# Gram-Schmidt rounds in the first half of each feed-forward pass, additions row by row, and a later turn in the last pass

## The chip, the cores and the metric

The kernel runs on one core of one Trainium2 chip. The metric is the device time of one execution in microseconds. The core has five engines with a queue of instructions each: TensorE (PE in the profile, with its weight loads as PEld), VectorE (DVE), ScalarE (ACT), GpSimd (POOL) and SyncE (SP). An engine takes its instructions in order; one that waits on a semaphore holds all behind it. DMAs are issued from a queue too, here nearly all from SP, a few from POOL. All arithmetic is in float32.

## The reference, cut to what matters

Eight sequences of 512 tokens with 512 features go through four layers:

```python
x = L0(x, ...)   # finite differences on a 512x512 grid, relu
x = L1(x, ...)   # attention with bias, then a feed-forward of 2048:
    h = _ln(x) * g2 + beta2
    ff = _gelu2(h @ W1 + b1) @ W2 + b2;      return x + ff
x = L2(x, ...)   # a feed-forward with weights of one expert per sequence:
    h = gelu(x @ Wi_b + bi_b);  r = h @ Wo_b + bo_b + x;  y = layernorm(r) * g_b + be_b
x = L3(x, ...)   # a low-rank edit:
    U_o = gram_schmidt(U);  V_o = gram_schmidt(V)      # U, V: 512 x 32
    basis = U_o @ V_o.T
    ...                                                # gate from the mean over tokens
    feats = (x @ basis) @ basis.T[:, :32]
    return x + strength * (feats @ resp_w.T + resp_b + safety_bias)
```

`gram_schmidt` is sequential over its 32 columns: column i is normalized, then its projection is taken from all later columns.

## The kernel before, in words

**Stages.** The grid of layer 0 takes the first 150 us or so, the attention of layer 1 runs to 1075 us, and then come sixteen feed-forward passes (`NQ = 2 * NB`): pass q = 0 to 7 is layer 1's feed-forward for sequence q, pass q = 8 to 15 is layer 2's expert feed-forward for sequence q - 8, followed by layer norm and layer 3 (the "tail"), most of which is done inside the next pass. The change is all in the feed-forward stage, `mlp_stage` (L1198).

**One pass.** A 128-partition tile `x` of 4 rows (R = 4) by 512 holds a sequence. Both matrix products of a pass are done with a seven-product scheme in place of eight block products, so that sums and differences of weight blocks (`w_quads`, `t13`, `t2s2`, `t4s4`, `r_sum`, on POOL by way of `gadd`) and of activation blocks (`b_staged`, `s13`, `l_sum`, on DVE by way of `add`, one operand staged into PSUM by ACT) have to be ready before the products that use them. `run(q, hooks)` (L1594) writes the pass:

- slots 0 to 27: four groups g of seven products u (slot 7g + m). Each is 8 matmuls of 128x256 into one of six PSUM buffers of tag `u`. The first product of a group is copied out by ACT, the others are added by DVE; then ACT applies the GELU, `gelu(1)` after product 5 and `gelu(0)` after product 6.
- slots 28 to 35 and 40 to 43: `second`, products y over all four groups. The first of them (y_28) reads, for group g, the first half of that group's activations, which `gelu(0)` writes; so its last 8 matmuls read what `gelu(0)` of the last group wrote.
- slots 36 to 39 and 44 to 55: `third`, four products split once more (named p2, p7, p3, p4, their tiles y_36, y_44, y_48, y_52). y_52a needs the DVE sums of p4, made at slots 47 to 49. In the last pass the fourth is replaced by two plain products, 52 and 54, each followed by `last_row`.

**The order is written by hand.** `hooks` maps a slot to a list of functions; `at(hooks, s, f, ...)` (L2139) appends one, and `go(s)` runs the list when the loop comes to that slot, before its matmuls. Every instruction is pinned to program order, so slot and place in the list set where it stands in each engine's queue. Hooks registered first stand first: at slots 7 and 14, `w_quads` is registered ahead of whatever Gram-Schmidt hook has the same slot.

**Gram-Schmidt.** The rows 0 to 31 of a 64x512 tile `qm` hold U transposed, rows 32 to 63 V transposed. Thirty-two rounds, four in each of passes 0 to 7, work on both at once:

- `gs_a(i)` (L1255): two DMAs on POOL's queue spread row i of either half over 32 partitions, into a tile `qb` (two buffers). 64 KB each.
- `gs_norm(i)` (L1265): on DVE two products with sums, of qb with itself (`junk_gn`) and of qm with qb (`junk_gd`), L1236; on POOL a square root as a power (L1243).
- `gs_b(i)` (L1270): on DVE the reciprocal (L1250, L1252), the coefficients `al` (L1275, L1276), the update of `qm` (L1277); and then it calls `gs_a(i + 1)`.

So round i + 1 can't begin before the DMAs of row i + 1 have landed, and these wait for the update of round i. After pass 7, `low_rank` (pass 8, slots 5 to 20) makes the low-rank weights of layer 3 out of `qm`.

**The rest that the change touches.** `add_row` (L1408) adds a bias row to all four rows of x on POOL. `add_beta` (L2023) adds layer 3's bias times the gate to a finished sequence in the tail, on POOL, and `tail_add` adds the response after it. `tail_turn` (L1969) turns 128 columns of the last pass's first two rows with two PE transposes and copies them out with ACT (L1983); the rows were scaled by DVE (L1934) at slot 50.

Of the kernel before, what the change touches and what calls it, by code (L numbers as in the profile page):

```python
# [22 lines left out]
D = 512  # L23
P = 128
R = 4
# [14 lines left out]
def fused_kernel(ctx: ExitStack, tc: tile.TileContext, a: dict):  # L40
# [172 lines left out]
    def load_late():  # L213
# [7 lines left out]
        g2, mhalf, load_w, load_late,  # L221
    )
    mlp_stage(tc, a, small, xp, io, wo8, x1d, ident, eidx, sigs, layernorm, rstd_of, phalf, wl3, g2, b1, first)


# [972 lines left out]
def mlp_stage(tc, a, small, xp, io, wo8, x1d, ident, eidx, sigs, layernorm, rstd_of, phalf, wl3, g2, b1, first):  # L1198
# [4 lines left out]
    with ExitStack() as ctx:  # L1203
# [15 lines left out]
        def gadd(out, x, y, op=ALU.add):  # L1219
            pin(nc.gpsimd.tensor_tensor(out, x, y, op))  # L1220
# [128 lines left out]
        wis, wos, xs, bts, tbs, wss, extra = {}, {}, {}, {}, {}, {}, {}  # L1349
# [57 lines left out]

        def add_row(q):  # L1408
            row = b2 if q < NB else extra[q][1][0]
            gadd(xs[q], xs[q], row[:, None, :].to_broadcast([P, R, D]))  # L1410

        hs, norms = {}, {}

# [26 lines left out]
        def rows32(q, r, src):  # L1440

            if r == 0:
                blks[q] = w8(wo8, f"tt_{q}").rearrange("p k d -> p (k d)").rearrange(
                    "p (n c r j) -> p c n r j", c=2, r=R, j=RK
                )
            pin(
                nc.vector.transpose(
                    blks[q][:, :, :, r, :], src.rearrange("p (c n j) -> p c n j", c=2, j=RK)
                )
            )  # L1450
# [572 lines left out]
        def add_beta(q):  # L2023
            x, st, beta = xs[q], outs[q]["st"], extra[q][1][2]
            pin(nc.vector.scalar_tensor_tensor(beta, rb, st, beta, ALU.mult, ALU.add))
            gadd(x, x, beta[:, None, :].to_broadcast([P, R, D]))

        def tail_sum(q, r):
            ft, m = outs[q]["ft"], slice(r * RK, (r + 1) * RK)
# [109 lines left out]
        def at(hooks, s, f, *args):  # L2139
            hooks.setdefault(s, []).append(lambda: f(*args))  # L2140
# [8 lines left out]
        for q in range(NQ):  # L2149
            hooks = {}  # L2150
            nx = q + 1 if q + 1 < NQ else None

            if q:
                at(hooks, 0, load_wi, q, 2)
                at(hooks, 0, load_wi, q, 3)
                at(hooks, 1, w_quads, q, 1, gadd)
            at(hooks, 0, load_wo, q)
            if nx:
                if nx >= NB:
                    at(hooks, 45, load_extra, nx)  # L2160
                at(hooks, 2, load_x, nx)
                at(hooks, 48, load_wi, nx, 0)
                at(hooks, 52, load_wi, nx, 1)
            if 1 <= q <= NB:
                at(hooks, 4, lambda q=q: nc.sync.dma_start(x2d[q - 1], xs[q - 1]))

            at(hooks, 2 if q else 26, add_row, q)
            at(hooks, 7, w_quads, q, 2, gadd)
            at(hooks, 14, w_quads, q, 3, gadd)
            for g in range(NG):  # L2170
                at(hooks, 18 + 2 * g, t13, q, g)
            if nx:
                if nx < NB:
                    at(hooks, 29, norm, nx)
                    at(hooks, 31, normed, nx)
                for r in range(R):
                    at(hooks, 34 + r, lambda r=r, n=nx: rows32(
                        n, r, hs[n][r] if n < NB else xs[n][:, r, :]
                    ))
                at(hooks, 38 if q <= NB else 40, turn, nx)  # L2180
                if nx < NB:
                    for c in range(KC):
                        at(hooks, 46 + c, scale, nx, c)
                at(hooks, 51, b_staged, nx)
                at(hooks, 51, w_quads, nx, 0, gadd)
            if q < NB:
                for i, s in enumerate((11 if q else 18, 25, 46, 51)):
                    at(hooks, s, gs_norm, 4 * q + i)
                    at(hooks, s + 2, gs_b, 4 * q + i)
            if q == 0:  # L2190
                at(hooks, 8, gs_a, 0)
                at(hooks, 10, load_constants)
                at(hooks, 38, constants)
            if q == NB:
                for i, s in enumerate((5, 11, 14, 16, 20)):
                    at(hooks, s, low_rank, i)
            elif q > NB:
                every = range(R)
                o = q - 1
                at(hooks, 5, tail_norm, o, every)  # L2200
                at(hooks, 9, tail_normed, o)
                for r in range(R):
                    at(hooks, 14 + 2 * r, lambda r=r, o=o: rows32(o, r, xs[o][:, r, :]))
                at(hooks, 28, tail_spread, o)
                for c in range(KC):
                    at(hooks, 34 + c, tail_scale, o, c)
                at(hooks, 37, tail_gamma, o, every)
                at(hooks, 38, tail_feats, o, every)
                at(hooks, 39, gate, o)
                at(hooks, 41, strength, o)  # L2210
                at(hooks, 42, add_beta, o)
                for r in range(R):
                    at(hooks, 46, tail_sum, o, r)
                    at(hooks, (47, 48, 49, 51)[r], tail_add, o, r)
            if q == NQ - 1:
                half = range(0, 2)
                at(hooks, 49, tail_norm, q, half)
                at(hooks, 50, tail_normed, q)
                for c in range(KC):
                    at(hooks, (51, 52, 53, 53)[c], tail_turn, q, half, [c])  # L2220
            run(q, hooks)


# [86 lines left out]
```

## Time and profile before

| | us |
|---|---|
| three runs | 2647.16, 2648.96, 2650.07 (median 2648.96) |
| the profiled execution | 2648.46 |
| its span, first to last instruction | 2646.5 |
| feed-forward stage | 1075 to the end |
| a pass with Gram-Schmidt (second and third) | 94.97 |
| the first pass | 102.4 (1074.94 to 1177.38) |
| pass 8 | 98.8 (1842.14 to 1940.95) |
| passes 9 to 14 | 97.67 each |
| in the third pass, busy: PE / DVE / ACT / POOL | 94.32 / 71.22 / 36.31 / 73.43 |

How to read it: "busy" is the time in which an engine worked; in the timelines an entry gives start, length, engine, line, operation, tiles written <- read, and in brackets how long the engine was idle just before and what ended that. In the waits "A x <- B y: total, times, longest" says that engine A waited before writing x for what B wrote in y. The page's slices show PE at nine tenths or more from the second slice on and a granted clock of nine tenths or more in all but the last; the mean granted clock is 0.994.

### The profile page before, as it was taken

The page shows a single profiled execution, that of the slowest core. Times are in us where ns is not written, and L with a number is a line of the kernel's source. Part 1 is how long each engine was busy: PE and PEld are TensorE (multiplying, and loading weights), DVE is VectorE, ACT ScalarE, POOL GpSimd, SP SyncE. Part 2 cuts the span into 40 slices and gives each one's busy share as a digit, 9 for nine tenths or more (in the row PEclk, how much of TensorE's full clock was granted, in tenths as well). Part 3 has the DMA queues.
Part 4 walks back from the last instruction along what each step waited for, and adds up shares of the span by engine and source line. Part 5 has one row for each costly group of instructions (what it writes and reads, how often), then busy time and mean ns, then how long its engine had stood idle before and what let it go on. Part 6 is the DMA issues. An engine that isn't in the chain of part 4 may idle for free.

```text
span 2646.5 us, 44047 instructions
## 1 busy us (share of the span) xinstructions
PE 2593.9 (98%) x15664; PEld 1968.5 (74%) x15664; DVE 1993.3 (75%) x3919; ACT 1311.1 (50%) x2748; POOL 1733.2 (65%) x1351
## 2 busy tenths in 40 slices
PE   6999999999999999999999999999999999999998
PEld 3455555555555555789899899898899899899897
DVE  7978898888888656587777777777667667667666
ACT  2676767777677766233334334333334434434433
POOL 4555565656555655478777777877776776776773
PEclk9999999999999999999999999999999999999998
DMA  9765766676666554543553563464245356256240
GB/s 327 255 228 184 263 199 232 216 242 220 238 222 227 174 188 166 142 137 96 166 180 68 152 197 74 128 189 138 108 161 179 108 184 199 89 187 214 74 174 34
DMA packets 241839, 460.59 MB, mean 174 GB/s; under 512 B 33904, under 2 KB 77496, under 8 KB 232534
## 3 DMA queue, kind: packets, MB, share of 16 engines
q1 hardware_dynamic: 237754, 447.04, 49.6%
q0 software_dynamic: 3552, 10.72, 3.8%
q8 instruction: 125, 2.05, 0.3%
q14 instruction: 92, 0.75, 0.1%
q10 hardware_dynamic: 316, 0.03, 0.0%
HBM read 398.43 MB, written 55.09 MB: 171 GB/s over the span
## 4 chain that ended last, share of the span: by engine, by line
PE 88%; DVE 7%; DMA 3%; issue 1%; ACT 1%; SPq 0%; POOL 0%; DVEq 0%; POOLq 0%; ACTq 0%
PE u L1211 28%; PE y L1211 12%; PE tr L564 8%; PE s L561 5%; PE ctx L561 4%; PE pv L561 4%; PE o L561 4%; PE pk L561 4%; PE pq L561 4%; PE y_36a L1211 2%; PE y_52a L1211 2%; PE y_36b L1211 2%; PE y_52b L1211 1%; PE y_44a L1211 1%; PE y_48a L1211 1%
## 5 line engine op out<-in xcount | busy, mean ns | idle before, releaser
L998 POOL TENSOR_TENSOR bt<-bt,mk 128x1024 f32<-128x1024 f32 x256 | 541.7, 2140 | 58.9 <-DMA bt<-in_bias 38.8
L1026 ACT ACTIVATE bt<-bt,mn 128x512 f32<-128x512 f32 x512 | 365.7, 718 | 80.1 <-DVE mn L1021 79.9
L564 PEld LDWEIGHTS tr<-ident,bt 128*128 128x128 f32 x2048 | 229.8, 141 | 149.4 <-issue 101.3
L1217 DVE TENSOR_TENSOR act<-u,u 128x512 f32<-128x512 f32 x256 | 175.4, 688 | 216.5 <-PE u L1211 186.0
L1021 DVE CUSTOM_DVE_ANT_0 bt<-s,bt 128x512 f32<-128x512 f32 x512 | 329.9, 684 | 4.7 <-PE s L561 4.1
L1211 PE MATMUL u<-bt,wi 128*128 128x256 f32 x1440 | 330.6, 379 | 0.0
L1052 ACT COPY pt<-tr 128x512 f32<-128x512 f32 x376 | 207.6, 584 | 204.9 <-PE tr L564 197.2
L1211 PEld LDWEIGHTS u<-bt,wi 128*128 128x128 f32 x1440 | 272.9, 190 | 35.9
L564 PE MATMUL tr<-ident,bt 128*128 128x128 f32 x2048 | 276.9, 278 | 7.6 <-ACT pt L1052 3.1
L1211 PE MATMUL u<-tb,ws 128*128 128x256 f32 x1024 | 242.3, 380 | 1.8 <-DVE yw L1217 1.8
L1211 PE MATMUL y<-t,s 128*128 128x256 f32 x1024 | 227.9, 380 | 0.0
L1211 PEld LDWEIGHTS u<-tb,ws 128*128 128x128 f32 x1024 | 194.6, 190 | 28.4 <-issue 2.1
L1211 PEld LDWEIGHTS y<-t,s 128*128 128x128 f32 x1024 | 193.2, 191 | 25.0
L1740 ACT ACTIVATE act<-act,b 128x512 f32<-128x512 f32 x128 | 85.3, 714 | 248.3 <-DVE act L1217 191.8
L1740 ACT ACTIVATE act<-act,bi 128x512 f32<-128x512 f32 x128 | 84.5, 713 | 239.0 <-DVE act L1217 239.0
L1050 DVE COPY pt<-tr 128x512 f32<-128x512 f32 x136 | 93.7, 689 | 134.8 <-PE tr L564 134.2
L1217 DVE TENSOR_TENSOR u<-u,u 128x512 f32<-128x512 f32 x192 | 131.3, 684 | 49.2 <-PE u L1211 48.2
L561 PE MATMUL s<-kt,qt 32*128 32x512 f32 x1024 | 165.7, 643 | 1.2 <-ACT kt L651 0.8
L1220 POOL TENSOR_TENSOR q<-wo,q 128x512 f32<-128x512 f32 x126 | 160.6, 1274 | 4.4
L1220 POOL TENSOR_TENSOR t<-wo,t 128x512 f32<-128x512 f32 x64 | 80.9, 1279 | 100.9 <-PE y L1211 100.9
L1502 ACT COPY st_s<-act 128x512 f32<-128x512 f32 x192 | 112.0, 589 | 70.4 <-DVE s L1217 32.2
L1220 POOL TENSOR_TENSOR wo<-wo 128x512 f32<-128x512 f32 x111 | 141.1, 1271 | 8.7
(440 smaller groups left out, 5575.5 us busy)
## 6 DMA issues: line engine op xcount, KB each, us to landing
bt<-in_bias SPq DMA_DIRECT2D x256, 512.0 KB
wo<-in_W SPq DMA_DIRECT2D x32, 1024.0 KB
wi<-in_Wi SPq DMA_DIRECT2D x32, 1024.0 KB
wo<-in_Wo_e SPq DMA_DIRECT2D x32, 1024.0 KB
wi<-in_W SPq DMA_DIRECT2D x28, 1024.0 KB
td<-tt SPq DMA_DIRECT2D x22, 1024.0 KB
bt<-td SPq DMA_DIRECT2D x176, 128.0 KB
gq<-coef_q SPq DMA_DIRECT2D x21, 512.0 KB
```

The lines of the kernel that those rows point to most:

```text
L561: pin(nc.tensor.matmul(out, lhsT=lhsT, rhs=rhs, start=start, stop=stop))
L564: pin(nc.tensor.transpose(out, src, ident))
L998: nc.gpsimd.tensor_tensor(bt, bt, mask[b, r][:, None, :].to_broadcast([P, 2, S]), ALU.add)
L1021: nc.vector.tensor_tensor_reduce(bt[:, i, :], ss[h], bt[:, i, :], -1.0, 3.0e38, ALU.add, ALU.min, mn)
L1026: nc.scalar.activation(bt[:, i, :], bt[:, i, :], AF.Exp, bias=mn, scale=-1.0, accum_out=sums[b, c][:, h, r : r + 1],)
L1050: pin(nc.vector.tensor_copy(pt[:, :, r % 2, :], tr))
L1052: pin(nc.scalar.copy(pt[:, :, r % 2, :], tr))
L1211: pin(nc.tensor.matmul(out, lhsT=lhsT, rhs=rhs, start=start, stop=stop))
L1217: pin(nc.vector.tensor_tensor(out, x, y, op))
L1220: pin(nc.gpsimd.tensor_tensor(out, x, y, op))
L1502: pin(nc.scalar.copy(t, parts[0]))
L1740: nc.scalar.activation(acts[:, g, k, :], acts[:, g, k, :], func, bias=bi[:, j : j + 1])
```

## The change

Three things are changed, and no arithmetic. (1) The four Gram-Schmidt rounds of a pass, which began at slots 11 (18 in pass 0), 25, 46 and 51 with `gs_b` two slots later, begin at 4 (6 in pass 0), 12, 17 and 23 with `gs_b` at 7 (9), 14, 19 and 25. In pass 0 the first `gs_a` goes from slot 8 to 1. (2) `add_row` and `add_beta` add four rows of 128x512 in place of one 128x2048, and `add_row` of pass 0 goes from slot 26 to 3. (3) In the last pass the four `tail_turn`s go from slots 51, 52, 53, 53 to 52, 53, 54, 55.

```diff
         def add_row(q):
             row = b2 if q < NB else extra[q][1][0]
-            gadd(xs[q], xs[q], row[:, None, :].to_broadcast([P, R, D]))
+            for r in range(R):
+                gadd(xs[q][:, r, :], xs[q][:, r, :], row)
...
         def add_beta(q):
             x, st, beta = xs[q], outs[q]["st"], extra[q][1][2]
             pin(nc.vector.scalar_tensor_tensor(beta, rb, st, beta, ALU.mult, ALU.add))
-            gadd(x, x, beta[:, None, :].to_broadcast([P, R, D]))
+            for r in range(R):
+                gadd(x[:, r, :], x[:, r, :], beta)
...
-            at(hooks, 2 if q else 26, add_row, q)
+            at(hooks, 2 if q else 3, add_row, q)
             at(hooks, 7, w_quads, q, 2, gadd)
             at(hooks, 14, w_quads, q, 3, gadd)
...
             if q < NB:
-                for i, s in enumerate((11 if q else 18, 25, 46, 51)):
+                for i, (s, e) in enumerate(((4, 7) if q else (6, 9), (12, 14), (17, 19), (23, 25))):
                     at(hooks, s, gs_norm, 4 * q + i)
-                    at(hooks, s + 2, gs_b, 4 * q + i)
+                    at(hooks, e, gs_b, 4 * q + i)
             if q == 0:
-                at(hooks, 8, gs_a, 0)
+                at(hooks, 1, gs_a, 0)
...
             if q == NQ - 1:
                 half = range(0, 2)
                 at(hooks, 49, tail_norm, q, half)
                 at(hooks, 50, tail_normed, q)
                 for c in range(KC):
-                    at(hooks, (51, 52, 53, 53)[c], tail_turn, q, half, [c])
+                    at(hooks, 52 + c, tail_turn, q, half, [c])
```

On the engines' queues the instructions of PE, ACT and DVE are the same in number; POOL has four additions for one in 23 places. On POOL's queue a pass from 1 to 7 now reads: w_quads 1, four row additions, power of round 0, w_quads 2, two DMAs, power of round 1, w_quads 3, two DMAs, power of round 2, t13 of group 0, two DMAs, t13 of groups 1 and 2, power of round 3, t13 of group 3, two DMAs.

## The prediction

> **What bounds the kernel now.** I read the page first, then the waits by engine, then the timelines of one ordinary pass (the third, 1272.35 to 1367.32), of the first pass, and of the last 50 us.
>
> ```profile
> PE 2593.9 (98%) x15664; PEld 1968.5 (74%) x15664; DVE 1993.3 (75%) x3919; ACT 1311.1 (50%) x2748; POOL 1733.2 (65%) x1351
> ```
>
> PE is the bound: 52.6 us of idle in the whole span, so a gain can only come out of the few PE waits, while a new PE wait is paid in full. The waits of PE in the feed-forward stage are these:
>
> ```profile
> PE y_52a L1211 <- DVE q L1217: 6.2, 8, 1.6
> ...
> PE y L1211 <- ACT act L1740: 2.6, 1, 2.6
> ...
> PE u L1211 <- DVE yw L1217: 1.8, 1, 1.8
> ...
> PE ytr L1214 <- DVE x L1934: 1.5, 1, 1.5
> PE y_44a L1211 <- DVE q L1217: 1.2, 1, 1.2
> ```
>
> The first is 1.63 in pass 0 and 0.65 in each of passes 1 to 7, the passes with Gram-Schmidt rounds; passes 8 to 15 don't have it. The second is in pass 0, the third at the start of pass 8, the fourth in the last pass.
>
> How a round is chained shows on POOL and DVE in the third pass (start, length, engine):
>
> ```profile
> 1316.99 0.95 POOL L1243 TENSOR_TENSOR gs_d<-gn_s,phalf 64x1 f32<-64x1 f32 x1 [3.02 <-DVE gn_s L1236]
> ...
> 1321.50 1.04 POOL L1259 DMA_DIRECT2D qb<-qm  x2 [1.08 <-DVE qm L1277]
> ...
> 1360.08 1.06 POOL L1259 DMA_DIRECT2D qb<-qm  x2 [5.59 <-DVE qm L1277]
> ```
> ```profile
> 1320.46 0.74 DVE L1277 SCALAR_TENSOR_TENSOR qm<-qb,al,qm 64x512 f32<-64x512 f32 x1
> ...
> 1367.73 0.68 DVE L1236 CUSTOM_DVE_ANT_0 junk_gn<-qb 64x512 f32<-64x512 f32 x1 [1.48 <-DMA qb<-qm]
> ```
>
> Issued at 1360.08, the row broadcast was usable at 1367.73: 7.65 us, with DVE standing still before it. For the broadcast issued at 1297.49 the tile view of qb gives
>
> ```profile
> DMA to landing us min/median/max: 4.6/5.2/5.7
> ```
>
> where 5.7 belongs to the second DMA, issued 0.54 later: 6.25 us from first issue to usable. Over all rounds it is 6.25 to 8.7 (1834.90 to 1843.61), the longer ones while weights are loading.
>
> **The deadline.** The last 8 matmuls of y_28 need the GELU of the last group's first half. Here it runs at 1321.84 and PE comes to them at 1320.70 + 5.18 = 1325.88. I count from a pass's first matmul (T = 1272.35): PE needs them at T+53.5. After the last round's gs_norm starts, the order on DVE is: gs_norm 1.22, u2 0.6, two s13 sums 1.2, u3 0.6, gs_b 1.51, two adds 1.2, one add 0.6; then on ACT two GELUs 1.33 and one 0.67, with 0.1 of handing over twice: 9.1. So **the fourth round's row must be there by T+44.4**, or PE waits.
>
> **Part 1, the rounds.** Removed: two rounds (2 x (1.22 + 1.51) on DVE) from slots 46 to 53 and the stand for the row at 51. Then the p4 sums end near T+87.2 (1362.3 less 2.7), before y_52a asks at T+88.6. All y_52a waits go: -6.2, of which 0.65 per pass 1 to 7. The start of pass 8 is no longer behind a late DVE: -1.8 (its 1.76 idle).
>
> Added: four rounds chained in slots 4 to 25. On POOL's queue each round is pow, then whatever stands before the two DMAs; at slots 7 and 14 w_quads is listed ahead of gs_b, so four gadds (4 x 1.235 = 4.94) come between pow and the DMAs; at slot 19 it is one t13 (2.5). Also, ops of DVE with two SBUF inputs were held while POOL worked: L1276 took 5.01 and 1.24 beside 0.15, L1277 1.72 beside 0.74, each until a POOL instruction ended. So:
> - Round 0: POOL has w_quads 1 from about T-1 (pass 9's row, 1939.91) and the four row adds until T+8.9; gs_norm at 7.6, held to about 8.85; pow until 10.6; w_quads 2 until 15.5. gs_b can start after the add of u_0_6, T+12.75; al held to 14.3, qm to 15.5, done 16.2. DMA 16.3, weight loads still running (here 0.69 to 1.05 busy until T+30): row there at 22.0 to 23.9, take 22.6. DVE comes to gs_norm at 21.95: almost no wait.
> - Round 1: pow ends at +1.7 (24.3), w_quads 3 then delays the DMAs to 29.3 without holds, 30.0 with them; row at 30.0 + 6.25 = 36.2. DVE stands for it from 31.2: 5 us, which the six u buffers cover (u_2_3 is read at 38.05, its buffer is wanted at slot 23, T+39.7; slack 1.7).
> - Round 2: 1.22, u3 0.6, two adds 1.2, gs_b 1.51 plus a hold to t13's end, DMA at 41.5: row at 47.7, **3.3 late**. A hold of 0.1 to 0.2 at round 3 makes the PE wait 3.5.
>
> Bounds: with no hold, the earliest landing and every row at its minimum, 21.95, 34.95 and 45.8: a wait of 1.4. With landings of 7.6 at the first hop and full holds: 49, a wait of 5.1. I take 3.5, since the 6.25 repeats in every round issued at slots 13 and 27 and POOL's order is fixed. PE also lost speed after such an idle: in pass 0, after 2.57 us, eight matmuls took 3.45 in place of 1.73 (granted clock 0.56 from 1131 to 1133); after 1.76 us in pass 8 only 0.1. So the clock adds 0.1 to 1.73; I take 1.73, the row nearest in length. Passes 1 to 7: 7 x (3.5 + 1.73 - 0.65) = **+32.1**.
>
> [...]
>
> [...]
>
> **Pass 0.** The broadcast moves from slot 8 to slot 1 but stands behind w_quads 1, which starts at T+6.4 (1081.35): issued T+11.5 and, with this pass's own 6.5 (row 1091.42), there at 18.0. From there the same hops: 31.8 (after w_quads 2), 45.0, 56.4, and GELU at 65.5, where PE here came at T+56.4 (1131.36): **+9.1**; the clock loss of 1.73 stands in both. DVE stands 6.6 us at slot 6, and PE waits at slots 18 and 23 for u buffers, inside that sum. With y_52a's 1.63 gone: +7.5. Low end +4, with the minimum hops; high +12, with busy landings.
>
> **Part 2, row additions.** A 128x2048 add is 4.55 on POOL (x23 here); four 128x512 are 4 x 1.235 = 4.94, so 0.4 more per pass on a POOL that idles 20 us of it: nothing on the path. What it does is to end DVE's holds sooner. Only pass 0 shows a long one, and it made the wait of 2.57:
>
> ```profile
> 1123.43 4.51 POOL L1220 TENSOR_TENSOR x<-x,b2row 128x2048 f32<-128x2048 f32 x1
> ```
> ```profile
> 1124.17 5.01 DVE L1276 TENSOR_TENSOR al<-al,below 64x1 f32<-64x1 f32 x1
> ```
> ```profile
> 1131.36 3.61 PE L1211 MATMUL y<-wo,act 128*128 128x256 f32 x8 [2.57 <-ACT act L1740]
> ```
>
> That gain is inside pass 0's +9.1. In add_beta the adds stay off the path (tail_add comes five slots, over 4.5 us, later). 0, between -1 and +1. SP issues nothing new.
>
> **Part 3, the last pass.** The turn of columns 0 comes after y_48b in place of before its last 14 matmuls. Those take 1.56 (14 x 0.1116), so PE reaches the turn at 2618.4 and the second row is scaled at 2618.75: the idle falls from 1.53 to 0.4. The clock loss (those 14 took 2.58 and the next eight 2.16 for 1.73) goes too: 1.1 + 1.0 + 0.4 = -2.5. The last turn, at slot 55, has 1.7 of matmuls behind it to cover its ACT copy (0.75). Between 0 and -3.
>
> **Sum**, against the profiled execution's 2648.46 (span 2646.5 and 2.0 around; 0.5 below the median of 2648.96): +32.1 + 7.5 - 1.8 - 2.5 = +35.3, **2684**. Ends: 7 x (1.4 + 0.1 - 0.65) + 4 - 4.3 = +6, 2655; 7 x (5.1 + 1.73 - 0.65) + 12 - 4 = +51, 2700.
>
> **Rivals.** *No new wait (faster).* Decided where the fourth row is there by T+44.4: the three hops would have to take 1.4 us less than my minimum together, for instance landings of 5.7. For it: DVE idles 14 of the 36 us between 1284 and 1320; against it: every landing in the trace is longer. Then -6.2 - 4.3 (pass 0's 2.57 and clock) - 1.8 - 2.5: 2633.7. *A wash:* a wait of some 0.7 without clock loss pays for y_52a: about 2648. *Worse:* the late DVE is not caught up by y_44a, as in pass 0, where `constants` (3.05 on DVE) left PE 1.2 short. For it: after the wait DVE's norm starts 0.3 (clock lost) to 2 us later against PE than here; against: pass 0's row leaves 3.05 - 1.2 = 1.8 us of room there. 7 x (5.1 + 1.73 + 1.2 - 0.65) + 12 - 4 = +60: 2708.
>
> **Chances.** Forecast 0.79, no new wait 0.09, wash 0.04, worse 0.08. The range reaches from the forecast's low end into the worse case: 2655 to 2708, leaving out about 0.17. A measurement tells 0.2% (5.3 us) from no change; faster 0.10, same 0.05, slower 0.85.
>
> **What would show it.** Right: PE y <- ACT act with 8 entries of 2 to 5 us where there is one; junk_gn <- DMA qb in the tens of us; no y_52a wait; passes 1 to 7 near 99.5 long in place of 94.97; a granted clock under 1 behind each wait; the last pass 2 to 3 shorter. Wrong: landings under 5 us, or POOL's pow and w_quads so early that DVE never stands at gs_norm, with passes of 94.3.

## The result and the profile after

| | before | after |
|---|---|---|
| median of the runs, us | 2648.15 (2645.22 to 2650.07, 6 runs) | 2710.48 (2705.97 to 2713.25, 6 runs) |
| ratio, 95% interval | 1 | 1.0233 (1.022 to 1.0246) |
| the profiled execution / its span | 2648.46 / 2646.5 | 2705.97 / 2704.2 |
| mean granted clock | 0.994 | 0.986 |

The change costs 62 us where 35 were forecast, and the time lies above the end of the range (2708). The busy line of the page of after:

```profile
PE 2613.7 (97%) x15664; PEld 1977.0 (73%) x15664; DVE 2025.0 (75%) x3919; ACT 1312.4 (49%) x2748; POOL 1750.2 (65%) x1420
```

PE has as many matmuls as before and is busy 20 us longer: it works at a lower clock for part of the time (mean 0.986 in place of 0.994). The rest of the loss is idle time. The waits of PE in after:

```profile
PE y L1211 <- ACT act L1741: 36.3, 8, 5.9
...
PE u L1211 <- DVE act L1217: 6.7, 2, 3.9
PE u L1211 <- DVE u L1217: 5.2, 3, 3.1
...
PE y_44a L1211 <- DVE q L1217: 1.2, 1, 1.2
...
PE ytr L1214 <- DVE x L2069: 0.4, 1, 0.4
```

The wait for the last GELU is there eight times, once in each pass with rounds; y_52a's wait and the old one of ytr are gone. The two lines of u are waits in passes 0 and 7 for a DVE that came late. By passes (from one pass's first matmul to the next, in us):

| | before | after | difference | forecast |
|---|---|---|---|---|
| ahead of pass 0 | 1074.8 | 1074.3 | -0.5 | 0 |
| pass 0 | 102.44 | 111.45 | +9.0 | +7.5 |
| passes 1 to 6 | 94.97 each | 100.1 to 102.1 | +37.1 | +27.5 |
| pass 7 | 94.97 | 112.75 | +17.8 | +4.6 |
| pass 8 | 98.81 | 96.81 | -2.0 | -1.8 |
| passes 9 to 14 | 97.67 each | 97.67 each | 0 | 0 |
| last pass | 119.74 | 116.03 | -3.7 | -2.5 |
| sum | | | +57.7 | +35.3 |

The sum is that of the profiled executions; that of after is the fastest of its six runs, so the medians stand 4.6 us further apart. An ordinary pass first, the third (T = 1286.64). POOL's queue, and the starts of the rounds on DVE:

```profile
1296.28 0.93 POOL L1243 TENSOR_TENSOR gs_d<-gn_s,phalf 64x1 f32<-64x1 f32 x1 [0.63 <-DVE gn_s L1236]
1297.19 1.27 POOL L1220 TENSOR_TENSOR ws<-wi 128x512 f32<-128x512 f32 x1
...
1303.11 1.06 POOL L1259 DMA_DIRECT2D qb<-qm  x2 [0.84 <-DVE qm L1277]
1311.72 0.95 POOL L1243 TENSOR_TENSOR gs_d<-gn_s,phalf 64x1 f32<-64x1 f32 x1 [7.56 <-DVE gn_s L1236]
1312.65 1.27 POOL L1220 TENSOR_TENSOR ws<-wi 128x512 f32<-128x512 f32 x1
...
1318.13 1.04 POOL L1259 DMA_DIRECT2D qb<-qm  x2
...
1329.90 1.05 POOL L1259 DMA_DIRECT2D qb<-qm  x2 [1.08 <-DVE qm L1277]
```
```profile
1310.94 0.69 DVE L1236 CUSTOM_DVE_ANT_0 junk_gn<-qb 64x512 f32<-64x512 f32 x1 [2.09 <-DMA qb<-qm]
1324.51 0.68 DVE L1236 CUSTOM_DVE_ANT_0 junk_gn<-qb 64x512 f32<-64x512 f32 x1 [5.07 <-DMA qb<-qm]
1336.31 0.68 DVE L1236 CUSTOM_DVE_ANT_0 junk_gn<-qb 64x512 f32<-64x512 f32 x1 [2.30 <-DMA qb<-qm]
```

Between a power (L1243) and the next two DMAs stand four weight sums. The rows go out at T+16.5, 31.5 and 43.3 (forecast 16.3, 30.0, 41.5) and are used at T+24.3, 37.9 and 49.7 (forecast 22.6, 36.2, 47.7). The prediction's T of 1272.35 stands 0.17 behind the first matmul in the timeline of before (1272.18), so 0.2 of each difference is the origin's. Of the 2.0 us missing at the end, 1.5 come from the first landing, which took 7.8 us while weights were loading and not 6.3; in the other five of passes 1 to 6 that landing took 6.5 to 6.9 and the last row was used at T+48.7 to 49.3. PE in the same pass:

```profile
1345.36 3.78 PE L1211 MATMUL y<-wo,act 128*128 128x256 f32 x8 [4.46 <-ACT act L1741]
```

And in four windows (behind the wait, the stretch after that, the wait itself, and later); the third column from the end is the granted clock:

```profile
1345.36:1349.14 3.78, 3.78 (x9) 3.06 (x10) 3.68 (x9) 1.56 (x3) 3.59 (x5) 0.50 0.20 8
1349.14:1352.30 3.16, 3.16 (x11) 2.61 (x11) 3.05 (x6) 1.70 (x3) 3.08 (x3) 0.71 0.00 0
1341.00:1345.36 4.36, 0.00 (x1) 0.00 (x1) 4.29 (x9) 2.00 (x4) 3.53 (x5) 0.86 0.73 23
1352.30:1356.00 3.70, 3.70 (x18) 3.24 (x18) 1.42 (x4) 3.70 (x7) 3.62 (x4) 1.00 0.00 0
```

The clock is 0.50 for the eight matmuls and 0.71 for 3.2 us more: 3.78 x 0.50 + 3.16 x 0.29 = 2.8 us lost, on top of the wait.

Pass 7 (T = 1792.59) is a case of its own. SP's queue and POOL's in after:

```profile
1786.57 0.40 SPq L231 DMA_DIRECT2D wi<-in_W  x1
1802.25 0.36 SPq L1395 DMA_DIRECT2D bo_e<-in_bo_e  x1
1802.72 0.92 SPq L231 DMA_DIRECT2D wi<-in_W  x2
```
```profile
1796.82 5.40 POOL L1220 TENSOR_TENSOR x<-x,b2row 128x512 f32<-128x512 f32 x4
1802.17 1.00 POOL L1243 TENSOR_TENSOR gs_d<-gn_s,phalf 64x1 f32<-64x1 f32 x1
1812.46 1.27 POOL L1220 TENSOR_TENSOR ws<-wi 128x512 f32<-128x512 f32 x1 [9.29 <-DMA wi<-in_W]
```

The bias row of the first expert (`bo_e`) shares its buffer with `b2row`, so its load has to wait for the row additions of pass 7, the last reader of `b2row`. In after it stands ahead of two weight loads of pass 7 on SP's queue; SP waits until the additions end at 1802.2, POOL stands 9.3 us for the weights, and the rounds queued behind the weight sums are late with them. In before the same load stood behind those weights:

```profile
1740.11 7.51 SPq L231 DMA_DIRECT2D wi<-in_W  x3
1747.67 6.71 SPq L235 DMA_DIRECT2D wo<-in_W  x4
1754.47 2.56 SPq L2165 DMA_DIRECT2D x2d<-x  x1
1762.69 0.36 SPq L1395 DMA_DIRECT2D bo_e<-in_bo_e  x1
```

The description of the kernel above says that every instruction is pinned to program order. That is not so: the weight loads (`load_wi`, `load_wo`) and `load_extra` are not pinned, and their places on SP's queue are found by the scheduler.

### The profile page after: what moved, and what is told of

Its sections match the earlier page's. It is cut to its first block, busy times and chain, and to the rows that moved or that the text cites. A ratio compares the mean times of both kernels' runs of the same rounds, so it can differ in the third digit from the quotient of the medians.

```text
span 2704.2 us, 44134 instructions
## 1 busy us (share of the span) xinstructions
PE 2613.7 (97%) x15664; PEld 1977.0 (73%) x15664; DVE 2025.0 (75%) x3919; ACT 1312.4 (49%) x2748; POOL 1750.2 (65%) x1420
## 4 chain that ended last, share of the span: by engine, by line
PE 78%; DVE 7%; DMA 6%; issue 5%; POOL 3%; ACT 1%; SPq 0%; DVEq 0%; POOLq 0%; ACTq 0%
PE u L1211 18%; PE y L1211 11%; PE tr L564 8%; PE s L561 5%; PE pv L561 4%; PE ctx L561 4%; PE pk L561 4%; PE pq L561 4%; DMA qb<-qm 3%; PE o L561 3%; PE y_44a L1211 2%; PE y_36a L1211 2%; PE y_52a L1211 2%; PE y_48a L1211 2%; POOL ws L1220 2%
## 5 line engine op out<-in xcount | busy, mean ns | idle before, releaser
L998 POOL TENSOR_TENSOR bt<-bt,mk 128x1024 f32<-128x1024 f32 x256 | 541.8, 2140 | 58.8 <-DMA bt<-in_bias 49.3
L1211 PEld LDWEIGHTS u<-tb,ws 128*128 128x128 f32 x1024 | 195.2, 192 | 41.5 <-DVE act L1217 8.5
L1211 PEld LDWEIGHTS y<-t,s 128*128 128x128 f32 x1024 | 197.4, 195 | 27.5
L1211 PE MATMUL y<-wo,act 128*128 128x256 f32 x544 | 135.9, 409 | 36.3 <-ACT act L1741 36.3
L1220 POOL TENSOR_TENSOR ws<-wi 128x512 f32<-128x512 f32 x60 | 76.3, 1272 | 126.0 <-DMA wi<-in_W 66.1
L1211 PEld LDWEIGHTS y<-wo,act 128*128 128x128 f32 x544 | 110.4, 205 | 55.8 <-ACT act L1741 39.5
```

Of the source, the lines that this page charges most:

```text
L998: nc.gpsimd.tensor_tensor(bt, bt, mask[b, r][:, None, :].to_broadcast([P, 2, S]), ALU.add)
L1211: pin(nc.tensor.matmul(out, lhsT=lhsT, rhs=rhs, start=start, stop=stop))
```

## The experiments

Theory: three causes, each a matter of one queue's order. In passes 1 to 6 the rows wait behind weight sums on POOL; in pass 7 weights wait behind `bo_e` on SP; in pass 0 four hops begin too late for the deadline. Rivals: DVE has too much to do in the first half, the landing through POOL's queue is long, or the row additions lengthen the chain.

**The parts of the change.** Two kernels: part 1 alone, and parts 2 and 3 alone (the lines of the diff above, nothing else).

> The kernel before with part 1 alone (the slots of the Gram-Schmidt rounds and of the first row broadcast). Theory: the slowdown is all part 1's. Then this kernel is slower than the changed one by what part 3 saves, 3.7 us in the last pass, and by what the long row addition does in pass 0: 2712 to 2722 us, passes 1 to 6 near 101.1, pass 7 near 112.8. Rival: the row-by-row additions, 5.40 us in place of 4.53 for each pass in the trace, lengthen the chain of rounds that stands behind them on POOL: then this kernel is several us faster than the changed one, below 2705, and passes 1 to 6 below 100.3.

Measured 2708.65 us, ratio 1.0228 (1.0212 to 1.0243): below the range that I expected, and as slow as the whole change. Passes 1 to 6 take 100.66 on average (after: 101.14), pass 0 takes 112.40 (111.45), pass 7 112.63 (112.75). So the loss is all part 1's, `bo_e`'s place too. The rival isn't borne out: the four row additions do take 5.4 in place of 4.53 ahead of the first round's power, but PE's wait for the last GELU is the same in both kernels (4.28 here, 4.31 in after, averages of passes 1 to 6). Of the 0.48 by which these passes are shorter here, 0.38 is the clock: it was low for 6.8 us in three of the six passes and for 3.4 in the other three, where after has four and two.

> The kernel before with parts 2 and 3 alone (row additions row by row, that of pass 0 at slot 3; turns one slot later). Theory: both are gains, hidden in the changed kernel under part 1's loss: the last pass falls by 3.7 us (119.7 to 116.0), and pass 0 by the wait of 2.57 and its clock loss of 1.73 that the long addition made: 2648 - 3.7 - 4.3 = 2640. Rival: the additions cost nothing and bring nothing, and another instruction holds DVE in pass 0: 2644.5.

Measured 2639.98 us, ratio 0.9968 (0.9956 to 0.998): the theory's number. Pass 0 takes 97.98 (102.44 before). The instruction that took 5.01 us beside the long addition takes 0.28 there:

```profile
1110.03 0.28 DVE L1276 TENSOR_TENSOR al<-al,below 64x1 f32<-64x1 f32 x1
1110.35 0.74 DVE L1277 SCALAR_TENSOR_TENSOR qm<-qb,al,qm 64x512 f32<-64x512 f32 x1
```

**The order on POOL.** The weight sums are registered behind the rounds of the same slot:

```diff
-            at(hooks, 7, w_quads, q, 2, gadd)
-            at(hooks, 14, w_quads, q, 3, gadd)
 ...
                     at(hooks, e, gs_b, 4 * q + i)
+            at(hooks, 7, w_quads, q, 2, gadd)
+            at(hooks, 14, w_quads, q, 3, gadd)
```

> The changed kernel with the weight sums of groups 2 and 3 listed behind the round of the same slot, so that on POOL the row broadcast goes out ahead of four additions (4.94 us) and not behind them. Theory (order of POOL's queue): each of two hops is 4 to 5 us shorter, the fourth row is there by about T+43 to 44, the wait of y for the GELU falls from 4.3 to at most 1 us in passes 1 to 6, which go from 101.1 to 94.3 to 96 each; pass 7 falls too, since its second row no longer stands behind the late weight sums; pass 0 gains one hop's 5. Time 2648 to 2668. Rival (DVE has too much to do in the first half, wherever the row stands): passes 1 to 6 stay above 99 and the time above 2693.

Measured 2670.88 us, ratio 1.0081 (1.0065 to 1.0096): 39.6 us less by the order of eight additions a pass, a little above the range expected. Pass 7 takes 103.26. Passes 1 to 6 take 96.0 to 97.3, with waits for the GELU of 1.0 to 2.4:

```profile
1437.49 1.99 PE L1211 MATMUL y<-wo,act 128*128 128x256 f32 x8 [2.22 <-ACT act L1741]
```

The rival of an overfull DVE is out for most of the loss. What is left is the first hop: sent at T+14.8 in the fourth pass (T = 1381.58), the row was used 9.6 us later, the next two 6.4:

```profile
1396.36 1.06 POOL L1259 DMA_DIRECT2D qb<-qm  x2 [4.69 <-DVE qm L1277]
...
1410.30 1.04 POOL L1259 DMA_DIRECT2D qb<-qm  x2 [2.59 <-DVE qm L1277]
...
1422.05 1.04 POOL L1259 DMA_DIRECT2D qb<-qm  x2 [1.08 <-DVE qm L1277]
```
```profile
1405.99 0.68 DVE L1236 CUSTOM_DVE_ANT_0 junk_gn<-qb 64x512 f32<-64x512 f32 x1 [2.20 <-DMA qb<-qm]
...
1416.67 0.68 DVE L1236 CUSTOM_DVE_ANT_0 junk_gn<-qb 64x512 f32<-64x512 f32 x1 [3.20 <-DMA qb<-qm]
...
1428.44 0.68 DVE L1236 CUSTOM_DVE_ANT_0 junk_gn<-qb 64x512 f32<-64x512 f32 x1 [2.29 <-DMA qb<-qm]
```

The fourth row is there at T+46.9 and PE waits 2.2, which puts the deadline at T+44.6; the prediction had T+44.4. Pass 0 gained only 1.6, not 5: its gs_b of slot 9 still stands behind the weight sums of slot 7, and the landing behind it took 8.3 us in place of 6.8 in after.

**The order on SP.**

```diff
-                    at(hooks, 45, load_extra, nx)
+                    at(hooks, 45 if nx > NB else 52, load_extra, nx)
```

> The changed kernel with the load of the first expert's small rows listed at slot 52 of pass 7 in place of 45, which puts it behind the weight loads of pass 7 on SP's queue. Theory (order of SP's queue): pass 7 no longer waits 9.3 us for its third weight tile and goes from 112.75 to the 100 to 102 of passes 1 to 6; the time falls by 11 to 13 to about 2698 and nothing else moves. Rival (pass 7 is longer because the first expert's loads crowd the DMA engines): no change, 2710.

Measured 2698.31 us, ratio 1.0185 (1.017 to 1.0201): 12.2 less, as expected. Pass 7 takes 102.41; passes 1 to 6 stay at 100.1 to 102.1. SP issues the two weights 0.7 us ahead of the pass's start (T = 1796.86), and `bo_e` only behind the first weights of pass 8:

```profile
1796.16 1.30 SPq L231 DMA_DIRECT2D wi<-in_W  x2
```

**Pass 0.**

```diff
-                for i, (s, e) in enumerate(((4, 7) if q else (6, 9), (12, 14), (17, 19), (23, 25))):
+                for i, (s, e) in enumerate(((4, 7), (12, 14), (17, 19), (23, 25)) if q else ((18, 20), (25, 27), (46, 48), (51, 53))):
 ...
-                at(hooks, 1, gs_a, 0)
+                at(hooks, 8, gs_a, 0)
```

> The changed kernel with the old slots for the rounds of pass 0 alone (18, 25, 46, 51, the first row sent at slot 8). Theory: pass 0's loss is its own four hops against the deadline, and with the rounds back it is 98.0 long in place of 111.45, as with parts 2 and 3 alone; the rest stays: 2697. Rival: the loss comes from the row additions at slot 3, in front of which or behind which the row is sent: pass 0 stays above 104, 2703 or more.

Measured 2695.25 us, ratio 1.0168 (1.0151 to 1.0185). Pass 0 takes 97.99. The row additions at slot 3 do no harm there; the four hops did. Pass 1 gets 3.4 longer (104.31), because its first row now leaves pass 0 at slot 53.

**All three together.**

> The changed kernel with three edits together, each run alone before: rows sent ahead of the weight sums, the first expert's small rows at slot 52, pass 0 on its old slots. Theory (three separate causes, what is left is the landing while weights load): 2710.5 - 12.2 (small rows) - 13.4 (pass 0) - 26 (six passes by 4.4) - 5 (pass 7 by what is left of it) + 3.4 (pass 1, its first row sent late) = 2657. Rival (they are one cause seen three times): the sum falls short by 10 or more, 2667 or more.

Measured 2654.91 us, ratio 1.0024 (1.0015 to 1.0033), as the theory had it. Alone they took off 39.6, 12.2 and 15.2, together 55.6 and not 67.0: two of them shorten the same pass 7 (112.75 to 103.26 and to 102.41 alone, 99.51 together), which makes 6.6 of the difference by the profiled executions, and two the same pass 0 (1.6). Pass 1, which paid 3.4 for the old pass 0 alone, doesn't pay here (97.44). What is left of the difference is no more than the several us by which medians and profiled executions differ. What is left over parts 2 and 3 alone is 15 us, in passes 1 to 6 (96.1 to 97.4) and 7.

**The row's DMA on another queue.** Both edits for POOL and SP, and the row broadcast on ACT's queue:

```diff
-                    nc.gpsimd.dma_start(
+                    nc.scalar.dma_start(
                         qb[o : o + RK, :], qm[o + i : o + i + 1, None, :].to_broadcast([1, RK, D])
                     )
```

> The changed kernel with both former edits (weight sums behind the round, small rows of the first expert at slot 52) and the row broadcasts issued on ACT's queue in place of POOL's. By the two former runs those edits alone give 2670.9 less some 6 in pass 7: about 2664, with waits of 1.0 to 2.4 us left in passes 1 to 6 (96.8 long). Theory (what is left is the transfer itself: in quiet 1.1 us to the first packet and 4.8 us of packets): another queue shortens little, passes 1 to 6 stay between 95.7 and 97, 2658 to 2666. Rival (POOL's queue makes the landing long): rows usable within 3 us of their issue, no wait left, passes 1 to 6 at 94.3 to 94.9 and about 2647.

Measured 2701.3 us, ratio 1.0199 (1.0184 to 1.0214): some 37 us above the 2664 that was estimated for the two edits alone, which neither theory nor rival had. ACT and DVE in the second pass (T = 1184.81):

```profile
1214.22 1.41 ACTq L1259 DMA_DIRECT2D qb<-qm  x2
...
1226.67 1.15 ACTq L1259 DMA_DIRECT2D qb<-qm  x2
...
1240.40 1.15 ACTq L1259 DMA_DIRECT2D qb<-qm  x2
1242.20 2.56 ACT L1741 ACTIVATE act<-act,b 128x512 f32<-128x512 f32 x4 [10.81 <-DVE act L1217]
```
```profile
1220.58 0.68 DVE L1236 CUSTOM_DVE_ANT_0 junk_gn<-qb 64x512 f32<-64x512 f32 x1 [1.81 <-DMA qb<-qm]
1224.91 1.73 DVE L1277 SCALAR_TENSOR_TENSOR qm<-qb,al,qm 64x512 f32<-64x512 f32 x1
1233.09 0.68 DVE L1236 CUSTOM_DVE_ANT_0 junk_gn<-qb 64x512 f32<-64x512 f32 x1 [1.46 <-DMA qb<-qm]
...
1238.65 1.72 DVE L1277 SCALAR_TENSOR_TENSOR qm<-qb,al,qm 64x512 f32<-64x512 f32 x1
```

The last of these updates in the same pass of the kernel with the rows on POOL's queue (T = 1187.07):

```profile
1238.57 0.74 DVE L1277 SCALAR_TENSOR_TENSOR qm<-qb,al,qm 64x512 f32<-64x512 f32 x1
```

The landing is the same (1214.22 to 1220.58 is 6.36, the next 6.42), so it is not POOL's queue that makes it long. The loss is on DVE: the update of qm takes 1.72 to 1.85 in all 32 rounds, in place of 0.74 where POOL stands waiting for it, and each row goes out later for it. Counted from the pass's first matmul, the fourth row is used at T+48.3 (T+47.0 with the rows on POOL's queue in the same pass), its update begins at T+53.8 (T+51.5), and the last GELUs start only at T+57.4. PE waits 5.4 to 6.2 for it, and passes 1 to 7 take 102.2 to 102.9. ACT's own queue isn't what makes the last wait: the GELUs start 0.7 us behind DVE's additions in both kernels. That POOL's additions are what holds DVE was not tried by itself, but the traces go with it: of the 64 updates of qm in before and after, the 17 that took 1.72 or 1.73 us (one in before, 16 in after) ran beside an addition of POOL, and the 47 that took 0.74 or 0.75 ran while POOL made none.

**Rounds that keep to the deadline.** Parts 2 and 3, the `load_extra` edit, and other slots. The first two of these kernels keep one round in the second half. Their slots for `gs_norm` and `gs_b` are (6, 8), (15, 17), (22, 24), (39, 41), and the same with (25, 27), (43, 45) as the last two; pass 0 has (13, 15), (20, 22), (26, 28), (45, 47).

> The kernel before with parts 2 and 3, and the rounds at slots 6, 15, 22 and 39 (13, 20, 26 and 45 in pass 0), the small rows of the first expert at slot 52: three rounds in the first half with 7 to 9 slots (12 to 16 us) between them, one where the row has time. Theory (it is the hop of 12 to 15 us against the deadline that costs, and rounds that keep to it are free): no wait of y for the GELU, none at y_52a; from 2640.0 down by 7 x 0.65 + 1.6 + 0.9 to about 2633. Rival: a round at slot 39 makes DVE late for the third sums, y_44a waits about 1 us in each pass: 2640 or more.

Measured 2648.02 us, ratio 1.0 (0.9991 to 1.0009). The rival's wait is there: y_44a waits 0.8 in each of passes 1 to 6 (95.2 long, for 94.97 in parts 2 and 3 alone); pass 7, where DVE has less to do (67.4 us busy in before, 71 in the others), has no such wait and takes 94.45. But most of the 8 us above parts 2 and 3 alone are pass 0's, which neither theory nor rival had: it took 104.5 in place of 97.98, since its rows there met the deadline no better than in after (a wait of 4.1 for the GELU).

> As the kernel with rounds at 6, 15, 22 and 39, but with the last two at 25 and 43. Theory: also about 2633. Rival: the round at slot 43 still stands before the p4 sums, and part of the wait at y_52a stays (0.3 to 0.65 us a pass): 2635 to 2638.

Measured 2648.07 us, ratio 1.0 (0.9992 to 1.0009). The wait moved to y_52a, 0.79 in each of passes 1 to 6, as the rival had it; the time is above both, since pass 0 took 105.3. With one or two rounds in the second half (two in before), PE waits 0.65 to 0.8 us in each of passes 1 to 6. So the first half is the better place, if the rows are in time. The next kernels begin at slot 2 and send the rows of passes 1 to 7 ahead of the weight sums of groups 2 and 3 and of the row additions:

```diff
+                plan = ((2, 3), (10, 12), (16, 17), (22, 23)) if q else ((18, 20), (25, 27), (46, 48), (51, 53))
 ...
+            early = 0 < q < NB
+            at(hooks, 6 if early else 2 if q else 3, add_row, q)
+            at(hooks, 4 if early else 7, w_quads, q, 2, gadd)
+            at(hooks, 13 if early else 14, w_quads, q, 3, gadd)
```

> The changed kernel with all four rounds of passes 1 to 7 still in the first half, but from slot 2 on (2, 10, 16, 22), each row sent ahead of the weight sums and of the row additions on POOL (these move to slot 6), the small rows of the first expert at slot 52, and pass 0 on the old slots of the rounds with its row additions at slot 3. Theory (only the deadline counts: the fourth row by T+44.4): rows sent at about T+8, 23 and 33, the fourth there at T+40, no wait left of y for the GELU or at y_52a, passes 1 to 7 at 94.3; pass 0 at 98.0 as with parts 2 and 3 alone: 2640.0 less 7 x 0.65 and 1.1 in pass 8: 2634. Rival (four rounds in the first half are more than DVE can hide there): waits of 0.5 us or more in passes 1 to 7 and 2638 or more.

Measured 2649.89 us, ratio 0.9999 (0.9987 to 1.001). This is in the rival's range, but mostly not for its reason: passes 2 to 6 take 95.2 to 95.6, pass 7 takes 96.6 (a wait of 2.2 for the GELU) and pass 1 takes 101.2, since its first row, sent at slot 53 of pass 0, isn't there at slot 2.

> As the kernel with rounds from slot 2, with the later rounds one slot earlier (2, 9, 15, 21). Theory: the rows set the pace, not the slots, so the same time within 1 us, about 2634, DVE standing one slot longer for each row. Rival: DVE's longer stands reach PE through the u buffers, 2637 or more.

(The later rounds at 9, 15 and 21, the weight sums of group 3 at slot 12.) Measured 2643.66 us, ratio 0.9979 (0.9966 to 0.9992). Passes 2 to 7 take 94.1 to 94.6, against 94.97 before; pass 1 takes 103.8, which puts the time above the theory's 2634. So one slot decided some 0.9 us in each of passes 2 to 6, more than the theory allowed. In passes 2 and 3, for instance, 0.3 to 0.4 of it are waits for the last GELU and at y_44a that are gone here; where the rest goes isn't settled.

> As the kernel with rounds at 2, 9, 15 and 21, but pass 1 on the slots 6, 15, 22 and 39, since its first row leaves pass 0 only at slot 53 and was not there at slot 2 (pass 1 took 103.84). Theory: pass 1 at 95.2, passes 2 to 7 at 94.1 to 94.6, pass 0 at 98.0, pass 8 at 96.8: by the lengths 0.2 more, 3.6 less and 1.1 less than parts 2 and 3 alone (2640.0): 2635.5. Rival: the saving of 0.5 a pass is lost to small waits elsewhere: 2640 or more.

(Pass 1 on 6, 15, 22 and 39, with its row additions and weight sums at their slots of after.) Measured 2636.89 us, ratio 0.9961 (0.9948 to 0.9975), near the theory's 2635.5 and the fastest of all, though its interval overlaps that of parts 2 and 3 alone. Pass 1 takes 97.0 and not 95.2: y_44a waits 2.6 there. Passes 2 to 7 take 94.1 to 94.4, but for one of 95.6. The rows of the fourth pass (T = 1361.67) on POOL and DVE:

```profile
1369.71 1.06 POOL L1259 DMA_DIRECT2D qb<-qm  x2 [2.02 <-DVE qm L1277]
...
1397.01 1.05 POOL L1259 DMA_DIRECT2D qb<-qm  x2 [3.80 <-DVE qm L1277]
```
```profile
1403.45 0.68 DVE L1236 CUSTOM_DVE_ANT_0 junk_gn<-qb 64x512 f32<-64x512 f32 x1 [3.55 <-DMA qb<-qm]
```

The first row is out at T+8.0, where after has T+16.5, and the fourth is there at T+41.8, ahead of the deadline. DVE still stands 3.55 us for it, and PE does not.

## Why the prediction was wrong, point by point

- **The mechanism** held: the fourth row late, PE waiting for the last GELU eight times, DVE standing 90.2 us for rows ("tens of us"), y_52a's wait gone, the clock down behind the waits. The deadline of T+44.4 was measured at T+44.6.
- **The step that failed most** is the half sentence "SP issues nothing new" in part 2. SP's instructions are the same in number, but part 1 moved one past two others: `bo_e` ahead of the weights of pass 7. It was read from the diff, and no step asked for SP's order. Pass 7 makes 13.2 us of the 22.4 missing; the kernel with `bo_e` later took back 12.2 of the time, and 10.3 in pass 7 (112.75 to 102.41). Why the scheduler placed it there isn't shown.
- **Passes 1 to 6** are 6.2 longer, not 4.6. The waits were 4.06 to 4.61, average 4.3, against 3.5 taken and within the bounds of 1.4 to 5.1: the first landing was sized by a quiet 6.3 and took 6.5 to 7.8 while weights load (and up to 9.6 in the kernel that sends it earlier). **The clock's loss** was taken from one row at 1.73, as the upper end; 6.2 less 4.3 plus the 0.65 of y_52a makes 2.5 a pass. It was mis-sized since that row had a low clock for 3.4 us, and here it was low for 6.8 us in four of the six passes. Together 9.6 us.
- **Pass 0**: rows at T+18.7, 33.1, 46.7 and 58.5 for a forecast of 18.0, 31.8, 45.0 and 56.4; +9.0 against +7.5, inside its bounds, though in part by luck: PE's idle time grew by 5.2 only, and the clock, whose loss was taken as unchanged, was low for 10.2 us in place of 3.4, which costs 3.4 more.
- **Pass 8** -2.0 for -1.8. **The last pass** -3.7 for -2.5; but that pass, unchanged, took 119.74 and 118.48 in two kernels, and with the later turns 115.2 to 117.2 in twelve, so the sign is sure and the size only roughly.
- **The rivals**: "worse" had a time near the one measured (2708), but not its reason. The late DVE did catch up by y_44a: that wait is there once, 1.2 in pass 0, as before. "No new wait" failed at the landings as the prediction said. It can be had, though, by sending the rows earlier, as the last kernels show; the prediction took POOL's order for given.
- **The landings and the clock.** The landings agree with the trace of before (6.25 and more from first issue to usable): 6.38 and more from first issue to use in the third pass of after. What a wait costs in clock doesn't follow from its length alone. No clock was lost behind one of 2.92 and one of 3.08 (eight matmuls in 1.97 and 1.99, kernel with part 1 alone), while the 2.57 of before and one of 2.79 in pass 0 of after were followed by eight matmuls in 3.61 and 3.78. The eight waits for the GELU in after, 4.06 to 5.94 long, were all followed by a lower clock (eight matmuls in 2.92 to 3.78). What sets the 2.92 and the 3.08 apart was not shown.

## What to carry to other kernels

When work is moved, read the order of every queue anew, also of those whose instructions the diff does not touch: here a load that nobody moved came to stand in front of two others, and cost some 12 us, most of it in one pass. A chain of small transfers is priced by what stands between the result and the issue, and by the landing under the loads of that very time (up to 9.6 us here), not by the landing in a quiet stretch (6.4). And a change with parts of both signs is worth taking apart: two of the three parts made the kernel 0.3% faster, and the third cost nothing any more in passes 2 to 7 once its rows went out first on POOL's queue (94.1 to 94.4 but for one of 95.6, against 94.97); passes 0 and 1 kept other slots there.

## What the runs showed of the hardware

- A row broadcast over 64 partitions from two single partitions (two DMAs of 64 KB) took 6.4 us from first issue to use in quiet, on POOL's queue and on ACT's alike: 6.38 and 6.41 in the third pass of after, where the DMA engines moved 21 and 23 GB/s, and 6.36 and 6.42 on ACT's queue. Beside weight loads it took up to 9.6: 7.83 in the same pass of after at 198 GB/s, 9.63 in the kernel with the rows sent first.
- The update of qm (L1277, DVE, two inputs in SBUF) took 0.74 where POOL stood waiting for it and 1.72 to 1.85 in all 32 rounds of the kernel with the rows on ACT's queue, where POOL went on with additions. A row's DMA on POOL's queue thus kept POOL quiet while DVE worked (idle for 1.08 until the update was done, ahead of the DMA at 1329.90 in after); moved to ACT's queue, it no longer did (an addition of POOL at 1199.13, 1.28 long, beside the update at 1199.22, 1.73 long).
- At some of PE's waits in before and after the granted clock fell to 0.50, for 3.4 or 6.8 us. In before it was low for 3.4 us (1131.25 to 1134.67), from the end of the wait of 2.57 in pass 0. In after, at the eight waits for the GELU (4.06 to 5.94), it was low for 6.8 us in passes 1, 2, 4, 5 and 7 and for 3.4 in passes 0, 3 and 6, and the eight matmuls that came next took 2.92 to 3.78 in place of 1.99. Half of that time is an estimated 1.7 or 3.4 us lost at most, less where PE stood idle in it. Behind the waits of 3.08 (ended at 1142.41) and 2.92 (ended at 1152.50) of the kernel with part 1 alone the clock stayed at 1.00. The wait of before with the time behind it, then the time behind the two waits of that kernel (after the window come its length and PE's busy time; third from the end is the clock):

```profile
1127.84:1131.25 3.41, 0.95 (x5) 0.50 (x3) 3.34 (x5) 0.66 (x2) 2.32 (x4) 1.00 0.00 0
1131.25:1134.67 3.42, 3.31 (x8) 2.68 (x9) 3.28 (x10) 1.67 (x4) 3.22 (x4) 0.50 1.18 38
```
```profile
1142.41:1144.40 1.99, 1.99 (x9) 1.78 (x10) 1.89 (x6) 1.55 (x3) 1.99 (x1) 1.00 0.41 14
1152.50:1154.50 2.00, 2.00 (x10) 1.79 (x11) 0.45 (x1) 2.00 (x4) 1.92 (x3) 1.00 0.00 0
```
